# First cross attention of a gated Flamingo block in float32: keys projected turned, two heads in 32 rows, four heads' products side by side

## The chip, the cores and the metric

The kernel runs on one core of a Trainium2 chip. A core has the engines TensorE (PE, with its weight loads PEld), VectorE (DVE), ScalarE (ACT), GpSimd (POOL) and SyncE (SP), each with its own instruction queue, and 16 DMA engines. SBUF and PSUM have 128 partitions ("rows"); a PSUM bank holds 512 float32 per partition. A `matmul` keeps `lhsT` (rows x columns) in the array as weights and streams the columns of `rhs` past it; operands may occupy only a part of the rows (a row group) and the result a part of the partitions (a column group). `64*128` in a profile line means 64 rows by 128 columns of the array.

The metric is device time in microseconds, the median of several executions. Beside it stands one profiled execution with its trace, whose own time differs a little from the median.

## The reference

Four batches of 256 tokens `x` (256 wide) pass two gated blocks, each a cross attention to 1601 context tokens (128 wide) and a feed-forward part; each of the four sub-blocks is `x = x + tanh(g) * f(layernorm(x))`. Only the first cross attention is changed:

```
y_dca, y_main = y[:, -16:], y[:, :-16]                 # 16 and 1585 context tokens
q = ln16(x @ Wq + bq)                                  # 16 heads of 16
k = ln16(y_main @ Wk + bk);  v = y_main @ Wv + bv
k_dca = ln16(...);           v_dca = ...               # from y_dca @ Wkv_dca + bkv_dca
ctx = softmax(q k^T / 4) v + softmax(q k_dca^T / 4) v_dca
return ctx @ Wo + bo
```

`ln16` is a layer norm over the 16 numbers of one head, with one weight and one bias vector of 16 for all heads. The weight `kn_w` and the factor 1/4 are folded into the queries; `kn_b` gives the same number for every key of a query (`qc`). The second cross attention (16 query heads of 128, 8 key heads), the mixture of 16 experts and the ternary feed-forward block follow.

## The kernel before

Everything is computed on one core in order: a preamble, the first cross attention, the experts, the second cross attention and the last feed-forward block. The stages overlap a little at their borders.

**Units of the first cross attention.** The loop runs over 16 slabs: 4 batches (b) x 4 slabs (s) of 4 heads. A slab has 14 slots (`TILES`), one for each pair of 128-key chunks and each pair of heads (r = 0 or 2). The keys of a batch, turned (a head's dimensions on the rows, keys along the columns), are made while the batch before is attended to; the batch's own buffers `kTs`, `vps` alternate.

**Numbers in three parts.** Queries and keys are held as three bfloat16 parts (`NP` = 3), whose sum is the float32 number. A key's head takes 64 rows (`RW`): three times 16 rows of parts and a row of ones against which the queries' shift stands. A score is the sum of three bfloat16 products over 64 rows. Two heads stand in the two halves of the 128 rows.

**Keys.** `key_project` (L471) multiplies a chunk of 128 context tokens with `wkv`, keys and values together (512 columns); DVE adds the bias, ACT copies the values into `vps`. `scale_heads` squares on ACT (L373), sums and takes the root on DVE, and multiplies on POOL (L384); `split` makes the parts with ACT copies (L346, L350) and subtractions on POOL (L347, L351); `key_turn` (L516) turns each chunk by a DMA transpose on SP's queue, 13 per batch. For the first batch the same is done in the preamble by `first_pair` (L484), `parts` (L852) and their helpers.

**Queries.** `query_project`, the same steps on DVE and POOL, `stage_queries` (POOL copies at L615), and `turn_queries` (L625, one DMA transpose), twice per slab: once without the shift for the greatest pass, once with it.

**Greatest scores.** `greatest_tile` (L643) computes queries x 384 keys for two heads and reduces them to their greatest (L650, DVE), 16 tiles per slab, one slab ahead of the attention; `shift` writes qc minus the greatest sum into the shift rows.

**Attention.** `attend_tile` (L682) computes 256 keys x 256 queries for two heads into a `ps_s` tile of two PSUM banks (three such tiles exist, shared with the greatest pass), and ACT takes the exponential into `e` (L690, 1024 columns). `weigh` (L704) multiplies the values, 17 columns of 32 per head with a column of ones, with `e`: four heads in four column groups of one PSUM tile; it runs every second slot for two chunks. At a slab's end `take` (L720) copies the sums out, `norm` (L725 to L733) turns them and divides, and after the last slab of a batch `turn` (L742) and `out_project` (L749 on) apply `wo`. `last_tokens` (L565 to L606) does the 16 extra tokens.

**Order.** `keep_order` pins each engine to the order in which the program issues its instructions. In a slot that order is: one or two greatest tiles (`COUNT`), attend, exponential, every second slot weigh, and then the steps that `plan`, a dictionary from slot to steps, has for it. Slots for the helpers come from fixed tables (`KEYS`, `PARTS_AT` and numbers in `plan_queries`). In the last batch, which has no next batch's keys to make, `load_feed_forward` fetches the experts' weights and `route` picks experts for the batches done.

Of the kernel before, what the change touches and what calls it, by code (L numbers as in the profile page):

```python
# [21 lines left out]
P = 128  # L22
# [37 lines left out]
def tile_gated_cross_blocks(ctx: ExitStack, tc: tile.TileContext, a: dict, out: bass.AP):  # L60
# [192 lines left out]
    NS, HS, RW, W, NP = H // 4, 4, 64, 32, 3  # L253
    VW = HD0 + 1
    KPAD = NKT * P
    kt_stack = ExitStack()
    ktp = kt_stack.enter_context(tc.tile_pool(name="kt", bufs=1))
# [4 lines left out]
    kTs_f = [ktp.tile([P, H // 2 * KPAD // 2], F32, name=f"kT{i}") for i in range(2)]  # L262
    with ExitStack() as ph:
# [3 lines left out]
        hp = ph.enter_context(tc.tile_pool(name="l0h", bufs=2))  # L267
        qp = ph.enter_context(tc.tile_pool(name="l0q", bufs=2))
        ps_s = ph.enter_context(tc.tile_pool(name="l0ps_s", bufs=3, space=PSUM))
# [3 lines left out]
        groups = [[0, 1, 2], [3, 4, 5], [6, 7, 8], [9, 10, 11], [12]]  # L273
        GN = 3

        def load_group(b, gi):

            k0 = groups[gi][0] * P
            n = min(GN * P, NMAIN - k0)
            t = fix.tile([P, GN * P], F32, name="ctxg", bufs=4)  # L280
            nc.sync.dma_start(out=t[:, :n], in_=a["ctxT"][:, b, k0 : k0 + n])
            return t
# [3 lines left out]
        bkv = wp.tile([P, 2 * D], F32, name="bkv")  # L286
        nc.sync.dma_start(out=wkv[:, :D], in_=a["L0_xattn_Wk"])
        nc.scalar.dma_start(out=wkv[:, D:], in_=a["L0_xattn_Wv"])
        fetched = {(0, 0): load_group(0, 0)}
        nc.scalar.dma_start(out=bkv[:, :D], in_=a["L0_xattn_bk"].partition_broadcast(P))  # L290
        load_x(0)
        nc.scalar.dma_start(out=bkv[:, D:], in_=a["L0_xattn_bv"].partition_broadcast(P))
        load_x(1)
        fetched[0, 1] = load_group(0, 1)
        wq = load(wp, "wq0", [P, DC, D], a["L0_xattn_Wq"].rearrange("(c p) n -> p c n", p=P), nc.scalar)
        bq = bcast_row(wp, "L0_xattn_bq", D, nc.scalar)
        fetched.update({(0, gi): load_group(0, gi) for gi in range(2, 4)})
        hn = {
            n: bcast_row(wp, f"L0_xattn_{n}", HD0, nc.sync if "dca" in n else nc.scalar)
            for n in ("qn_w", "qn_b", "kn_w", "kn_b", "kn_dca_w", "kn_dca_b")  # L300
        }
        early = ph.enter_context(ExitStack())
        lp = early.enter_context(tc.tile_pool(name="l0last", bufs=1))
# [4 lines left out]
        bdca = bcast_row(lp, "bkv_dca", 2 * D)  # L308
        load_gates()
        wo = load(wp, "wo0", [P, DC, D], a["L0_xattn_Wo"].rearrange("(c p) n -> p c n", p=P))  # L310
        bo = bcast_row(wp, "L0_xattn_bo", D)
        for t in range(QT, NT):
            load_x(t)

        kTs = [t.bitcast(BF16).rearrange("p (c k) -> p c k", c=H // 2) for t in kTs_f]
        vps = [fix.tile([P, NKT, H * VW + W - VW], F32, name=f"vp{i}") for i in range(2)]
        kps = [fix.tile([P, GN, H, RW], BF16, name=f"kp{i}") for i in range(2)]
        kp_last = fix.tile([P, 1, H, RW], BF16, name="kp_last")
        qps = [fix.tile([P, NP, QT, HS, RW], BF16, name=f"qp{i}") for i in range(2)]
        nc.gpsimd.memset(kp_last, 0.0)  # L320
        for t, n in ((kps[0], P), (kps[1], P), (kp_last, TMAIN)):
            nc.gpsimd.memset(t[:n, :, :, NP * HD0 :], 0.0)
            nc.gpsimd.memset(t[:n, :, :, NP * HD0 : NP * HD0 + 1], 1.0)
        for t in qps:
            nc.gpsimd.memset(t[:, :, :, :, NP * HD0 :].rearrange("p n i h e -> p (n i h) e"), 0.0)

        def center(t3):

            g = t3.shape[1]
            sm = small.tile([P, 2 * H], F32, name="cen", bufs=2)  # L330
            nc.vector.reduce_sum(sm[:, :g], t3, axis=AX.X)
            nc.vector.tensor_scalar_mul(sm[:, :g], sm[:, :g], 1.0 / HD0)
            nc.vector.tensor_tensor(t3, t3, bc_last(sm[:, :g], HD0), ALU.subtract)
# [8 lines left out]
        def split(dsts, src, eng, first_eng=None):  # L342


            def first():
                nc.scalar.copy(dsts[0], src)  # L346
                (first_eng or eng).tensor_tensor(src, src, dsts[0], ALU.subtract)  # L347

            def second():
                nc.scalar.copy(dsts[1], src)  # L350
                eng.tensor_tensor(dsts[2], src, dsts[1], ALU.subtract)  # L351

            return [first, second]
# [12 lines left out]
        def scale_heads(src, n, g):  # L366

            sq = hp.tile([P, GN * H, HD0], F32, name="sq", bufs=1)
            v = small.tile([P, GN * H], F32, name="hn_var", bufs=2)[:n, :g]
            y, t = (small.tile([P, GN * H], F32, name=f"hn_{k}", bufs=1)[:n, :g] for k in "yt")  # L370

            def square():
                nc.scalar.activation(sq[:n, :g], src, AF.Square)  # L373

            def variance():
                nc.vector.reduce_sum(v, sq[:n, :g], axis=AX.X)
                nc.vector.tensor_scalar(v, v, 1.0 / HD0, 1e-6, ALU.mult, ALU.add)

            def root():
                log_root(v, y)  # L380
# [83 lines left out]
        def key_project(b, gi, ctxg, kns, i):  # L464
# [3 lines left out]
            if i == 0:  # L468
                kns[gi] = hp.tile([P, GN * H, HD0], F32, name="kn")
# [1177 lines left out]
```

## Time and profile before

| | us |
|---|---|
| median of 3 executions | 1617.81 (1617.75 to 1618.63) |
| profiled execution | 1620.98 |
| its span in the trace | 1619.3 |
| first exponential of the attention loop (L690) | 80.33 |
| last `take` (L720) of the first cross attention | 575.5 |
| from there to the end of the span | 1043.8 |
| mean granted TensorE clock | 0.981 |

The time from one `take` to the next, from first exponential on, adds up by batch to 142.4, 131.0, 127.0 and 94.9 us.

A page of the profile gives each engine's busy time in us, its share of the span and its instructions. A group line reads: line, engine, operation, output <- inputs, shapes, count | busy time, mean ns of one | idle time of the engine just before them and what ended it. A float32 matmul appears as two records, a bfloat16 one as one; records of matmuls overlap, since they are pipelined. A line of waits reads: engine and operation <- what it waited for: total us, times, longest us. A line of the chain of waits that ended last gives start, length, engine and line. A timeline line gives start, length, engine, line, operation, shapes, and in brackets the idle time before it.

### The profile page before, as it was taken

The numbers are of one execution on the slowest core, as the hardware profiler recorded it, in microseconds if no ns is written. First come the engines' busy times: TensorE is split into PE (matmuls) and PEld (weight loads), VectorE is DVE, ScalarE is ACT, GpSimd is POOL, SyncE is SP. The second block draws the span as 40 slices with busy tenths as digits, with TensorE's granted clock in tenths as the row PEclk, the third lists the DMA queues.
The fourth block names the chain that finished last, engine by engine and source line by source line (L and its number), as shares of the span: only waits on it lengthen the run. The fifth ranks groups of instructions, "written<-read, shape, count | busy, mean of one in ns | idle before, by whom it ended". The sixth has DMA issues, their size and how long they took to land.

```text
span 1619.3 us, 33935 instructions
## 1 busy us (share of the span) xinstructions
PE 1539.1 (95%) x13282; PEld 924.2 (57%) x13282; DVE 1159.3 (72%) x2615; ACT 798.9 (49%) x1852; POOL 601.7 (37%) x538
## 2 busy tenths in 40 slices
PE   4599999999999999989999999999999999999998
PEld 1354554554555545446666666666666666666665
DVE  6867677768767536687777777777777777777655
ACT  3256546556654634344455555544445454455343
POOL 4513213312401234434445444454444444444410
PEclk8799999999999989999999999999999999999999
DMA  4522414413442140000000000000000000000000
GB/s 113 110 45 48 73 33 68 83 26 54 84 87 54 41 166 1 1 2 9 8 16 15 15 9 15 9 22 2 15 15 9 22 9 15 9 2 3 2 0 27
DMA packets 148464, 54.04 MB, mean 33 GB/s; under 512 B 133200, under 2 KB 143952, under 8 KB 148176
## 3 DMA queue, kind: packets, MB, share of 16 engines
q1 hardware_dynamic: 134592, 50.65, 14.9%
q10 hardware_dynamic: 13712, 1.23, 0.6%
q8 instruction: 104, 1.70, 0.4%
q14 instruction: 56, 0.46, 0.1%
HBM read 24.30 MB, written 1.05 MB: 16 GB/s over the span
## 4 chain that ended last, share of the span: by engine, by line
PE 80%; DVE 11%; ACT 3%; issue 3%; POOL 2%; DMA 1%; ACTq 0%; SPq 0%; DVEq 0%; POOLq 0%
PE ps_o L1424 21%; PE ps_sc L1361 20%; PE ps_s L682 7%; PE ps_s L643 6%; PE ps_o L704 5%; PE ps_y L1442 4%; DVE mxs L650 4%; PE ps_m L1350 3%; PE ps_m L471 2%; PE ps_v L1184 2%; ACT pr L1376 1%; PE ps_a L1198 1%; PE ps_g L1555 1%; PE ps_x L1129 1%; PE ps_u L1555 1%
## 5 line engine op out<-in xcount | busy, mean ns | idle before, releaser
L1411 POOL TENSOR_TENSOR pr<-pr,rs 128x1604 f32<-128x1604 f32 x128 | 364.0, 2866 | 435.1 <-DMA rs<-ws 419.6
L1424 PE MATMUL ps_o<-pT,cx 128*128 128x256 f32 x1664 | 372.9, 382 | 7.8 <-DVE pT L1417 7.8
L1368 DVE CUSTOM_DVE_ANT_0 pr<-ps_sc,mk 128x401 f32<-128x401 f32 x512 | 294.7, 577 | 96.0 <-PE ps_sc L1361 57.3
L1361 PE MATMUL ps_sc<-ctxT,qT 128*32 128x401 f32 x4096 | 359.5, 502 | 0.5 <-DVE nm L1368 0.5
L1376 ACT ACTIVATE pr<-pr,nm 128x401 f32<-128x401 f32 x512 | 321.2, 628 | 71.2 <-DVE nm L1368 70.6
L1424 PEld LDWEIGHTS ps_o<-pT,cx 128*128 128x128 f32 x1664 | 318.9, 192 | 52.1 <-DVE pT L1417 8.5
L650 DVE TENSOR_REDUCE mxs<-ps_s 128x2 f32<-128x768 f32 (+1 forms) x256 | 245.5, 979 | 75.8 <-PE ps_s L643 75.2
L690 ACT ACTIVATE e<-ps_s 128x1024 f32<-128x1024 f32 (+1 forms) x224 | 214.7, 964 | 163.2 <-PE ps_s L682 150.5
L1417 DVE STREAM_TRANSPOSE pT<-pr 128x1664 f32<-128x1664 f32 x128 | 242.9, 1899 | 4.7 <-POOL pr L1411 4.7
L1361 PEld LDWEIGHTS ps_sc<-ctxT,qT 128*32 128x32 f32 x4096 | 126.4, 110 | 204.2 <-issue 118.6
L643 PE MATMUL ps_s<-kT,qTs 64*128 64x384 bf16 (+1 forms) x1536 | 173.7, 339 | 33.3 <-DMA qTs<-qp 18.1
L682 PE MATMUL ps_s<-qTs,kT 64*128 64x256 bf16 x2496 | 173.6, 270 | 9.5 <-DVE mxs L650 9.3
L682 PEld LDWEIGHTS <-kT 64*128 64x128 bf16 x2496 | 125.0, 94 | 54.9 <-issue 21.7
L643 PEld LDWEIGHTS <-qTs 64*128 64x128 bf16 x1536 | 65.2, 96 | 128.7 <-issue 82.0
L704 PE MATMUL ps_o<-e,vp 128*32 128x256 f32 x1664 | 112.6, 389 | 0.0
L1393 ACT ACTIVATE ws<-ws 32x32 f32<-32x32 f32 x64 | 14.6, 228 | 193.3 <-DVE ws L1392 193.3
L1434 ACT COPY ao<-ps_o 128x256 f32<-128x256 f32 x64 | 23.9, 373 | 152.8 <-PE ps_o L1424 141.4
L1376 ACT ACTIVATION_READ_ACCUMULATOR pr<-pr,nm 128x1 f32 x512 | 95.5, 186 | 0.0
L1442 PE MATMUL ps_y<-vo,ao 128*128 128x256 f32 x256 | 72.9, 408 | 1.9 <-ACT ao L1434 1.9
L1442 PEld LDWEIGHTS ps_y<-vo,ao 128*128 128x128 f32 x256 | 43.6, 190 | 46.3 <-ACT pr L1376 39.9
L704 PEld LDWEIGHTS ps_o<-e,vp 128*32 128x32 f32 x1664 | 44.6, 110 | 42.0 <-issue 24.7
L1350 PE MATMUL ps_m<-xnT,aq 128*128 128x256 f32 x256 | 65.8, 380 | 0.0
(287 smaller groups left out, 1507.3 us busy)
## 6 DMA issues: line engine op xcount, KB each, us to landing
ctxT<-in_ctxT_dram SPq DMA_DIRECT2D x4, 800.5 KB, 7.7
ctxg<-in_ctxT_dram SPq DMA_DIRECT2D x16, 192.0 KB, 3.1
kT<-in_L_xattn_Wq_dram SPq DMA_DIRECT2D x4, 512.0 KB, 3.6
wo<-in_L_xattn_Wo_dram SPq DMA_DIRECT2D x4, 512.0 KB, 4.8
bq<-nm SPq DMA_DIRECT2D x128, 2.0 KB, 1.7
bq<-nm ACTq DMA_DIRECT2D x128, 2.0 KB, 2.0
rs<-ws SPq DMA_DIRECT2D x128, 1.0 KB, 1.9
rs<-ws ACTq DMA_DIRECT2D x128, 1.0 KB, 1.8
```

The costliest lines, as they stand in the source:

```text
L643: nc.tensor.matmul(ps[:, k, :w], lhsT=qT[rows, j, i, r, :], rhs=kT[rows, 2 * s + r, c0 : c0 + w], start=j == 0, stop=j == NP - 1,)
L650: nc.vector.tensor_reduce(greatest_of[u][:, i, 2 * r : 2 * r + 2, n], ps[:, :, :w], AX.X, ALU.max)
L682: nc.tensor.matmul(ps[:, k, jj * S : (jj + 1) * S].rearrange("p (i q) -> p i q", i=QT), lhsT=kT[rows, 2 * s + r // 2, (j + jj) * P : (j + ...
L690: nc.scalar.activation(e[:, :, : nj * S], ps[:, :, : nj * S], AF.Exp)
L704: nc.tensor.matmul(summed[u][(r + k) * W : (r + k + 1) * W, :S], lhsT=vps[b % 2][:, j + jj, h * VW : h * VW + W], rhs=made[u, j, r][:, k, ...
L1361: nc.tensor.matmul(ps[i * TQ : (i + 1) * TQ, :KS], lhsT=queries[u][:, t * TQ : (t + 1) * TQ], rhs=ctxT[b][:, i * KS : (i + 1) * KS], start ...
L1368: nc.vector.tensor_tensor_reduce(out=prs[u % 3][:, t, :KS], in0=ps[:, :KS], in1=masks[b], scale=-1.0, scalar=3.0e38, op0=ALU.add, op1=ALU. ...
L1376: nc.scalar.activation(p, p, AF.Exp, bias=found[u][:, 0, t : t + 1], scale=-1.0, accum_out=found[u][:, 1, t : t + 1])
L1411: nc.gpsimd.tensor_tensor(p, p, bc_last(factors[:, ts], KS), ALU.mult)
L1417: nc.vector.transpose(pTs[u % 2][:, ts].rearrange("p t k -> p (t k)"), prs[u % 3][:, ts].rearrange("p t k -> p (t k)"))
L1424: nc.tensor.matmul(po[:, u % 2], lhsT=contexts[b][:, k, :], rhs=pTs[u % 2].rearrange("p t (k q) -> p t k q", q=TQ)[:, :, k, :], start=k == ...
L1442: nc.tensor.matmul(ys[b][:, i], lhsT=outs[u][:, i * P : (i + 1) * P], rhs=vo[:, h, :], start=(h, i) == (0, 0), stop=(h, i) == (H - 1, QT - 1),
```

## The change

Only the first cross attention and its preamble change (L250 to L1020); what follows is the same code.

- **Float32 throughout.** There are no parts: one float32 product over 16 dimensions takes the place of three bfloat16 ones over 64 rows. A head has 16 rows, two heads share 32 rows (even and odd slabs by turns, the other head's rows zeroed in the queries), and the four heads of a slab lie in four row groups.
- **Keys projected turned.** `key_product` (L472 after) has the centred weights `wk` stationary and up to 397 context tokens moving, so keys arrive with dimensions on the rows: eight products a batch. ACT squares them (`key_square`), ACT or DVE writes the raw keys (`key_raw`), `key_roots` (L502) sums squares by products with `hsum` and takes roots on DVE, `key_scale` (L525) spreads the roots over the rows by products with `sel`, and DVE multiplies. Values have their own products, `value_project` (L535). No DMA transposes remain.
- **Shift in a freed row.** Centred keys of a head add up to zero, so the 16th dimension can be dropped if it is subtracted from the queries' other 15 (`stage_queries`, L652 on); its row of keys is one and its row of queries the shift.
- **Queries turned by TensorE.** `turn_queries` (L664) is two PE transposes and an ACT copy.
- **Wider greatest tiles.** Three chunks of 453 keys and a rest of 226 keys for both query halves: 14 tiles per slab (L688), reduced at L697/L699.
- **Order in a slot.** attend (L732, two row groups), then a greatest tile of a slab ahead for the other two row groups, then the exponential (L742), then weigh for one 128-key chunk (L757, each slot), then the plan's steps. `book` gives at most one step that uses the `ps_m` tile to a slot; helpers are placed by it. `ps_s` still has three tiles; `e` has five (four before).
- **Preamble.** It does the keys of batch 0 by `first_keys`, then scales only the first half of the heads; the rest of the values and the extra tokens are interleaved with the first slab's greatest tiles. Context tokens are loaded whole, four DMAs per batch.

```diff
-    NS, HS, RW, W, NP = H // 4, 4, 64, 32, 3
+    NS, HS, W = H // 4, 4, 32
+    HW = H // 2
+    NG = 4
+    KG = (NMAIN + NG - 1) // NG
...
-    def key_project(b, gi, ctxg, kns, i):
-            nc.tensor.matmul(pm[:n], lhsT=ctxg[:, i * P : i * P + n], rhs=wkv, start=True, stop=True)
...
-    def key_turn(b, gi):
-                nc.sync.dma_start_transpose(
-                    out=kTs[b % 2][:, :, t * P : t * P + n],
-                    in_=parts_of(gi)[:n, i].rearrange("p h e -> p (h e)"),
-                )
+        def key_product(b, c, g, ps):
+            k0, n = GROUPS[g]
+            nc.tensor.matmul(ps[:, :n], lhsT=wk[:, c], rhs=ctxs[b][:, k0 : k0 + n], start=True, stop=True)
+        def key_square(c, g, ps):
+            nc.scalar.activation(sq[:, c, k0 : k0 + n], ps[:, :n], AF.Square, bias=kbias[:, c : c + 1])
+        def key_raw(b, c, g, ps, eng):
+            if eng is nc.scalar:
+                nc.scalar.activation(dst, ps[:, :n], AF.Identity, bias=rbias[:, c : c + 1], scale=n15)
+            else:
+                eng.tensor_scalar(dst, ps[:, :n], n15, rbias[:, c : c + 1], ALU.mult, ALU.add)
+        def key_roots(b):
+            for c in range(2):
+                for g in range(NG):
+                    nc.tensor.matmul(pm[g * W : (g + 1) * W, :KG], lhsT=hsum[:, c],
+                        rhs=sq[:, c, g * KG : (g + 1) * KG], start=c == 0, stop=c == 1)
+            nc.vector.tensor_scalar(v, pm[:, :KG], epsc, None, ALU.add)
...
+        def key_scale(b, c, half):
+            ps = ps_s.tile([P, 2, 512], F32, name="ps_s")
+            for i in range(2):
+                g = 2 * half + i
+                rows = slice(g * W, (g + 1) * W)
+                nc.tensor.matmul(ps[:, i, :KG], lhsT=sel[rows, c], rhs=roots[b][rows], start=True, stop=True)
+            nc.vector.tensor_tensor(k3, k3, ps[:, :, :KG], ALU.mult)
+        def value_project(b, t0):
+                nc.tensor.matmul(pm[:n, k], lhsT=ctxs[b][:, k0 : k0 + n], rhs=wv, start=True, stop=True)
...
-            nc.sync.dma_start_transpose(
-                out=t.rearrange("p n i r q -> p (n i r) q"), in_=qps[s % 2].rearrange("p n i h e -> p (n i h e)")
-            )
+        def turn_queries(u, k):
+            for i in range(QT):
+                nc.tensor.transpose(pt[:, i * P : (i + 1) * P], qps[slabs[u][1] % 2][:, i].rearrange(...), ident)
+            nc.scalar.copy(t, pt[:, :S])
...
-            for j in range(NP):
-                for k in range(2):
-                    rows = slice(k * RW, (k + 1) * RW)
+            for m, ii in enumerate([i] if whole else range(QT)):
+                for k in range(2):
+                    rows = slice((r + k) * W, (r + k + 1) * W)
...
-                for n in range(NP):
-                    for k in range(2):
-                        rows = slice(k * RW, (k + 1) * RW)
+                for k in range(2):
+                    rows = slice((r + k) * W, (r + k + 1) * W)
+                    nc.tensor.matmul(
+                        ps[:, k, jj * S : (jj + 1) * S],
+                        lhsT=kT[rows, s // 2, (j + jj) * P : (j + jj + 1) * P],
+                        rhs=qT[rows], start=True, stop=True)
+            def exponentials():
+                nc.scalar.activation(e[:, :, : nj * S], ps[:, :, : nj * S], AF.Exp)
...
-                for _ in range((COUNT if u else FIRST_COUNT)[k]):
-                    if todo:
-                        v, g = todo.pop(0)
-                        greatest_tile(v, *g)
-                attend_tile(u, k)
-                if k % 2 == 1 and k > 1:
-                    weigh(u, *PAIRS[k // 2 - 1])
-                run(plan, base_slot + k)
+                exponentials = attend_tile(u, k)
+                if ahead:
+                    v, _ = ahead.pop(0)
+                    next_greatest(v, 2 - TILES[k][2])
+                exponentials()
+                t = k - 2
+                if t >= 0:
+                    weigh(u, t)
+                elif t == -2 and u > 0:
+                    weigh(u - 1, NKT - 1)
+                for step in plan.pop(u * SLOTS + k, []):
+                    step()
```

## The prediction

> **What bounds the kernel now.** I read the page first: busy time, chain by line, groups. Its lines hold the whole program; only those at L643 to L704 belong to the 1st cross attention's loop.
>
> ```profile
> PE 1539.1 (95%) x13282; PEld 924.2 (57%) x13282; DVE 1159.3 (72%) x2615; ACT 798.9 (49%) x1852; POOL 601.7 (37%) x538
> ...
> L650 DVE TENSOR_REDUCE mxs<-ps_s 128x2 f32<-128x768 f32 (+1 forms) x256 | 245.5, 979 | 75.8 <-PE ps_s L643 75.2
> L690 ACT ACTIVATE e<-ps_s 128x1024 f32<-128x1024 f32 (+1 forms) x224 | 214.7, 964 | 163.2 <-PE ps_s L682 150.5
> ```
>
> Then the busy time of each engine by stretch: the preamble (up to the first exponential), the four batches, and all that follows. The columns are busy time and instructions of PE, PEld, DVE, ACT and POOL, then clock, DMA share and GB/s.
>
> ```profile
> 0.00:80.19 80.19, 41.04 (x206) 19.95 (x206) 58.19 (x99) 22.90 (x38) 41.38 (x84) 0.81 0.51 109
> 80.19:222.60 142.41, 132.22 (x1535) 72.12 (x1535) 101.87 (x195) 78.46 (x122) 32.57 (x52) 0.98 0.33 56
> 222.60:353.60 131.00, 125.83 (x1511) 69.17 (x1512) 97.66 (x189) 76.21 (x117) 33.15 (x54) 1.00 0.32 57
> 353.60:480.60 127.00, 122.79 (x1502) 67.97 (x1504) 95.07 (x180) 75.57 (x115) 32.45 (x53) 1.00 0.35 66
> 480.60:577.00 96.40, 94.77 (x1324) 57.82 (x1321) 53.75 (x128) 56.32 (x71) 16.05 (x35) 1.00 0.25 59
> 577.00:1619.30 1042.30, 1022.48 (x7211) 637.14 (x7210) 752.77 (x1828) 489.46 (x1389) 446.11 (x260) 0.99 0.06 15
> ```
>
> TensorE is busy 93 to 98% of the four batches: they are bound by its stream. The preamble is not: DVE, its busiest engine, works 58.2 of 80.2 us, and the clock is 0.81. The waits up to 80.2 us, longest first, say why:
>
> ```profile
> PE ps_s L643 <- DMA qTs<-qp: 18.1, 1, 18.1
> ...
> POOL kT L852 <- DVE v L364: 12.6, 2, 10.8
> ...
> PE ps_s L643 <- DMA kT<-kp: 3.6, 1, 3.6
> ```
>
> So 21.7 us of the preamble PE waits for DMA transposes. Last, the prices of products, from the chain around 730 us and the timelines at 641, 322 and 323 us:
>
> ```profile
> 729.28 5.53 PE ps_sc L1361 x64
> ...
> 735.86 5.61 PE ps_o L1424 x26
> ```
>
> ```profile
> 641.06 0.69 PE L1184 MATMUL ps_v<-xlT,kT 64*128 64x512 f32 x1
> ...
> 641.06 0.69 PE L1185 MATMUL ps_g<-xlT,kT 64*128 64x512 f32 x1
> ...
> 641.59 0.59 PE L1184 MATMUL ps_v<-xlT,kT 64*128 64x512 f32 x1
> ...
> 641.60 0.59 PE L1185 MATMUL ps_g<-xlT,kT 64*128 64x512 f32 x1
> ```
>
> ```profile
> 322.30 0.60 PE L682 MATMUL ps_s<-qTs,kT 64*128 64x256 bf16 x8
> ...
> 323.00 1.02 ACT L690 ACTIVATE e<-ps_s 128x1024 f32<-128x1024 f32 x1 [2.09 <-PE ps_s L682]
> 323.20 0.66 PE L643 MATMUL ps_s<-kT,qTs 64*128 64x384 bf16 x6
> ...
> 323.70 0.82 PE L682 MATMUL ps_s<-qTs,kT 64*128 64x256 bf16 x12
> ```
>
> A float32 product leaves two records. L1424's 26 records are 13 products of 256 columns: 5.61/13/256 = 1.69 ns per column. L1361's 64 are eight rounds of four 401-column products in four column groups: 0.69 a round, 1.72 per column, so four abreast cost what one does. L1184 and L1185, in two halves of the rows, begin together and take the same time: rows stand abreast as well. In bf16, twelve L682 products are six pairs, and less a record of 0.27 us, (0.82-0.27)/5 = 0.11 per pair; L643's three 384-wide pairs, (0.66-0.33)/2 = 0.16. An exponential starts 0.10 us after the last product's record ends (322.90 to 323.00).
>
> **The change: the stream.** Per batch, before: 624 L682 products are 312 pairs, 34.3 us; 384 L643 ones 192 pairs, 30.7; sum 65.0. After: attend (L732) is 104 float32 pairs of 256, 0.433 each, 45.0 us; the greatest pass (L688) 56 tiles of 453 columns, 0.766 each, 42.9. One behind the other that is 87.9, worse by 23. But attend takes two row groups and the greatest tile issued next the other two; abreast they would need about 45, better by 20. How far they overlap is set by the score buffer.
>
> **The change: the slot's wait.** Three buffers, two tiles per slot: the greatest tile of slot k takes the buffer of attend k-1, so it waits for that exponential. Attend is 0.107 (first load) + 2 x 0.433 = 0.97. Its exponential ends at 0.97 + 0.17 (record past stream, 0.27-0.11) + 0.10 + 1.02 = 2.26; PE goes on 0.16 after a ScalarE release (copy L595 ends 324.29, L599 starts 324.45). The greatest tile lasts 0.107 + 0.766 = 0.87. Weigh (L757) now comes each slot: switch of tile shape 0.09 + load 0.03 + 0.433 = 0.55, and 0.09 back (the gaps around L704 are 0.09). With m the inserted PE steps of a slot, slot k+1 begins m later than the later of a(k)+0.97+0.55+0.09 = a(k)+1.62 and a(k-1)+2.26+0.16+0.87+0.55+0.09 = a(k-1)+3.94. If the second always decides, a slot is 1.97 + m/2. Behind the waiting greatest tile stand weigh and all helpers on PE's queue; DVE and ACT then wait for them.
>
> **m.** Each step is load 0.107 + columns x 1.69 ns + switch 0.094. Per batch: key products 8 x 0.87 = 7.0, roots 1.5, four scale products 2.3, seven value steps 7.5, two query steps 2.1, new PE transposes of queries 8 x 0.42 = 3.4 (were DMAs), other transposes 10 x 0.42, last tokens 4.2, output 2.1: some 33, 0.6 per slot. Before, keys with values were 13 x 1.07 = 13.9, now 18.3; with the query transposes 7.8 us more PE work a batch, and 24 more visits to the weigh shape (52 for 28), 24 x 0.19 = 4.6 us. A slot is then 2.27 on average; carried slot by slot with each slot's own helpers (larger-of does not average) the batches come to 130.0, 129.6, 129.6 and 109.9 = 499.0. Before they were 142.4, 131.0, 127.0 and 94.9 to the last take at 575.5, sum 495.3. So the loop gets 3.7 slower: the first batch gains, where POOL's splits and DMA turns held up keys, and the last loses 15, since bf16 needs no second pass there and four rows abreast have no greatest tile beside them. The last slab, 23.6 by this, might be 20.5 if its exponentials run free; I leave it.
>
> **Other engines in the loop.** The reduce widens from 768 to 906 elements: L650 took 950 ns and, for 866 elements, 1057, so about 1.10, against 1.10/2.27 of the slot: hidden. Exponentials stay 1.02 of 2.27: hidden, except through the buffer. ACT gains squares, raw keys and query copies (0.37 each), POOL loses splits and copies: hidden by slack of 50% or more; if ACT's helpers run ahead of an exponential, it is late by 0.4, and half of that goes to its slot. SP loses 52 key and 32 query transposes, and its context loads become four a batch (five before), issued a slab or more ahead of use; at a DMA share of 0.33 nothing waits.
>
> **Preamble.** The DMA turns go (21.7 us of waits), the splits and most of POOL with them. Next late is DVE: 94 instructions, 47 us by the rows of before (18 greatest tiles 19.7). Bounds for the first exponential: 47 x 58.2/62.3 (its durations sum to 62.3) + the same 22 idle = 66; and 80, if the idle time comes back as waits on PE copies. I take 71, below their middle, since the waits that go are the longest: -9.
>
> **Tail.** L1 and the FFNs are unchanged, the 1043.8 us behind the last take stay; weights for the FFN are issued in the last batch before and after.
>
> **Sum.** -9 + 3.7 = -5.3. Span 1619.3 to 1614.0, the profiled execution 1621.0 to 1615.7; the median stands 3.2 below that execution: 1612.5.
>
> **A rule against it.** The trace has two row groups abreast, not four. It has four results at the same rate, though: an L682 pair yields two columns per 0.43 ns, four float32 tiles four per 0.85. So I take full overlap. The Trainium skill, "TensorE: Matmul & The Clock Gate", Part 3 (Packing small matmuls), gives 3.07 times, not 4, for four 32-row tiles of 512 columns. By it row tiles would be 30% slower, the recurrence would give 554 instead of 499, and the median would be about 1668; no row here shows it.
>
> **Rivals.** (1) Slower, the other side: four 32-row tiles are not fully abreast. For: never seen in this trace; against: the pair and the four column groups. In the recurrence 5% on L688 and L732 gives +9 (1622), 10% gives +18 (1631), pairs one after the other +113 (1726). Break-even is 3%. (2) The score buffer is freed later, because ACT helpers stand before the exponential or the release takes longer: 0.14 us per slot gives +9, 1622; for: ACT is busier per slot than the 58% of before; against: the idle time before L690. (3) No gain in the preamble: DVE's waits move to the PE turns; 1618 to 1621. (4) Cheaper: switches hidden under the buffer wait (0.05 instead of 0.094) give -19, 1593; no wait for the exponential at all -35, 1578, for which the fourth buffer is missing. (5) The change doesn't do what it says: TensorE keeps program order over row groups, so greatest and attend follow each other. The timeline at 598 us, where an L1185 of the next expert starts before an L1184 that precedes it, speaks against; it would be rival 1's +113.
>
> **How the numbers follow.** Forecast (1604 to 1616 by preamble bounds) 0.46; rival 4 0.14; rival 3 0.10; rivals 1 and 2 together 0.28, 5 0.02. Within 0.2% (3.2 us, about what a measurement of this kernel can tell from no change) lies rival 3 and the forecast's edge: same 0.13; faster 0.57; slower 0.30. The range drops the 35-us gain, the 30% case and serial pairs: 1593 to 1632.
>
> **What would show it.** Right: first exponential near 71 us with no DMA wait at the greatest tiles; exponentials 2.1 to 2.4 us apart; the last take near 570; PE in the greatest line waiting for ACT's e; L688 and L732 beginning together in four row groups; 1043.8 us after the last take. Wrong: L732 rounds longer than 0.433 per 256 columns when a greatest tile is beside them (rival 1), exponentials starting over 0.3 us after their products (rival 2), or a first exponential at 78 or later (rival 3).

## The result, and the profile after

The changed kernel takes 1617.26 us (median of 12, 1615.52 to 1624.2), the kernel before 1619.63 (12 executions, 1614.68 to 1623.44). The ratio, worked out over the single executions and not from the two medians, is 0.9995, with a 95% interval of 0.9979 to 1.0012: no difference that this measurement can tell. The forecast was 1612.5 us. The twelve executions of the changed kernel run from 1615.5 us at a mean granted clock of 0.983 (five of them within 0.5 us) to 1624.2 at 0.977, and the one profiled, at 0.978, is among the five longest.

That execution (1621.13 us, span 1619.4) shows that the equality is a sum of unequal parts:

| part | before, us | after, us | difference | forecast |
|---|---|---|---|---|
| up to the first exponential | 80.33 | 79.07 | -1.3 | -9 |
| first exponential to last take | 495.2 | 499.8 | +4.6 | +3.7 |
| behind the last take | 1043.7 | 1040.6 | -3.1 | 0 |

A second trace of the kernel before, at the end of the experiments, has 82.36, 491.9 and 1042.5 us; against it the differences would be -3.3, +7.9 and -1.9.

From the page of the changed kernel, busy times and the groups that answer to those of before:

```profile
PE 1566.6 (97%) x12200; PEld 915.5 (57%) x12200; DVE 1100.0 (68%) x2409; ACT 795.3 (49%) x1837; POOL 514.2 (32%) x424
...
L697 DVE TENSOR_REDUCE mxs<-ps_s 128x2 f32<-128x906 f32 x192 | 210.4, 1100 | 139.7 <-PE ps_s L732 70.0
L742 ACT ACTIVATE e<-ps_s 128x1024 f32<-128x1024 f32 (+1 forms) x224 | 215.2, 963 | 174.8 <-PE ps_s L732 156.3
...
L688 PE MATMUL ps_s<-kT,qT 32*128 32x453 f32 (+1 forms) x1024 | 232.3, 563 | 2.1 <-ACT e L742 1.2
```

The reduce takes 1.10 us, as worked out, and DVE and POOL lose work; TensorE gains 27 us of busy time, a part of it from products at half clock. By stretch (preamble, the four batches, the rest; columns as before):

```profile
0.00:79.07 79.07, 51.87 (x194) 24.74 (x196) 45.06 (x94) 19.88 (x39) 14.43 (x58) 0.74 0.26 74
79.07:212.66 133.59, 132.70 (x1246) 67.79 (x1246) 83.44 (x121) 77.01 (x113) 12.79 (x24) 0.96 0.03 7
212.66:342.13 129.47, 127.20 (x1242) 65.39 (x1243) 82.63 (x126) 75.77 (x110) 12.96 (x25) 1.00 0.01 1
342.13:471.61 129.48, 127.22 (x1242) 65.41 (x1244) 82.62 (x126) 75.77 (x111) 12.95 (x25) 1.00 0.04 10
471.61:578.85 107.24, 106.11 (x1073) 55.56 (x1071) 55.05 (x113) 59.30 (x76) 15.02 (x32) 1.00 0.11 32
578.85:1619.40 1040.55, 1021.49 (x7218) 636.62 (x7218) 751.21 (x1829) 487.58 (x1390) 446.09 (x260) 0.99 0.06 16
```

A batch is counted from its first exponential to that of the next, the last one to the last `take`, here as in the times by batch of the kernel before. The middle batches come to 129.5 us, where the recurrence, the prediction's slot-by-slot sum, said 129.6; the first to 133.6 (130.0), the last to 107.2 (109.9). In the preamble DVE and POOL are relieved as forecast (45.1 and 14.4 us of work), but TensorE's busy time *grew*, from 41.0 to 51.9, at a clock of 0.74 instead of 0.81. A finer cut shows where:

```profile
50.00:55.00 5.00, 3.12 (x15) 1.74 (x16) 4.79 (x9) 3.79 (x6) 1.83 (x3) 1.00 0.00 2
55.00:60.00 5.00, 4.23 (x16) 1.94 (x15) 1.15 (x2) 0.85 (x2) 2.84 (x9) 0.50 0.00 0
60.00:65.00 5.00, 4.32 (x22) 2.53 (x21) 1.84 (x5) 0.59 (x1) 1.32 (x6) 0.50 0.00 0
65.00:70.00 5.00, 3.50 (x13) 1.40 (x6) 3.51 (x9) 0.36 (x1) 0.00 (x0) 0.50 0.46 130
70.00:75.00 5.00, 4.00 (x16) 1.77 (x16) 0.72 (x1) 0.74 (x2) 0.00 (x0) 0.50 0.09 32
75.00:80.00 5.00, 5.00 (x24) 2.94 (x24) 4.08 (x5) 0.93 (x1) 0.00 (x0) 0.50 0.00 0
80.00:85.00 5.00, 5.00 (x26) 2.56 (x24) 2.58 (x3) 1.49 (x3) 0.00 (x0) 0.50 0.01 3
```

The granted clock is 0.50 from 55 us on; finer cuts have it back at 89.2. That takes in the last two of the seven rounds of the first slab's greatest tiles, the query turns, the second slab's first greatest tiles and the first four slots of the attention. The chain of waits says what came just before:

```profile
50.89 1.28 ACT L991
52.17 0.01 issue
52.18 0.21 ACT gate L991
52.39 0.02 issue
52.41 1.28 ACT L992
53.69 0.01 issue
53.70 0.59 ACT vp L536
54.30 0.04 issue
54.34 1.46 PE ps_m L535 x4
```

The gate's tanh, with a table load before and one after it (L991, L992), stands ahead of a value copy on ScalarE's queue. The value product L535 needs the bank that this copy frees, so TensorE stood idle for 1.88 us up to 54.34; the half clock begins at 55.0. That the one causes the other is only a theory so far.

Four row groups do stand abreast. The timeline of TensorE in a slot of the second batch:

```profile
243.80 0.48 PE L732 MATMUL ps_s<-qT,kT 32*128 32x256 f32 x2
243.82 0.65 PE L688 MATMUL ps_s<-kT,qT 32*128 32x453 f32 x2
244.12 0.38 PE L732 MATMUL ps_s<-qT,kT 32*128 32x256 f32 x2
244.31 0.55 PE L688 MATMUL ps_s<-kT,qT 32*128 32x453 f32 x2
244.33 0.60 PE L732 MATMUL ps_s<-qT,kT 32*128 32x256 f32 x4
```

All eight attend records precede the greatest tile's four in program order, yet L688 begins 0.02 us after the first L732 and before the other six. Attend and greatest tile end together after 1.1 us; one behind the other they would need 0.97 + 0.87 = 1.84.

### The profile page after: what moved, and what is told of

Same layout as the page of the kernel before. It is cut to its first block, busy times and chain, and to the rows that moved or that the text cites. A ratio compares the mean times of both kernels' runs of the same rounds, so it can differ in the third digit from the quotient of the medians.

```text
span 1619.4 us, 31284 instructions
## 1 busy us (share of the span) xinstructions
PE 1566.6 (97%) x12200; PEld 915.5 (57%) x12200; DVE 1100.0 (68%) x2409; ACT 795.3 (49%) x1837; POOL 514.2 (32%) x424
## 4 chain that ended last, share of the span: by engine, by line
PE 88%; DVE 4%; ACT 3%; issue 3%; POOL 1%; DMA 1%; ACTq 0%; SPq 0%; DVEq 0%; POOLq 0%
PE ps_o L1433 21%; PE ps_sc L1370 20%; PE ps_s L732 9%; PE ps_o L757 7%; PE ps_s L688 7%; PE ps_y L1451 4%; PE ps_m L1359 3%; PE ps_v L1193 2%; PE ps_m L535 2%; PE ps_m L472 1%; ACT pr L1385 1%; PE ps_a L1207 1%; PE ps_m L664 1%; DVE mxs L697 1%; PE ps_g L1564 1%
## 5 line engine op out<-in xcount | busy, mean ns | idle before, releaser
L697 DVE TENSOR_REDUCE mxs<-ps_s 128x2 f32<-128x906 f32 x192 | 210.4, 1100 | 139.7 <-PE ps_s L732 70.0
L742 ACT ACTIVATE e<-ps_s 128x1024 f32<-128x1024 f32 (+1 forms) x224 | 215.2, 963 | 174.8 <-PE ps_s L732 156.3
L732 PE MATMUL ps_s<-qT,kT 32*128 32x256 f32 x1664 | 240.1, 405 | 1.0 <-ACT e L742 0.9
L688 PE MATMUL ps_s<-kT,qT 32*128 32x453 f32 (+1 forms) x1024 | 232.3, 563 | 2.1 <-ACT e L742 1.2
L732 PEld LDWEIGHTS ps_s<-qT,kT 32*128 32x128 f32 x1664 | 142.2, 186 | 73.1 <-issue 39.7
L757 PE MATMUL ps_o<-e,vp 128*32 128x256 f32 x1664 | 134.3, 392 | 0.6 <-ACT e L742 0.6
L688 PEld LDWEIGHTS ps_s<-kT,qT 32*128 32x128 f32 x1024 | 80.1, 192 | 11.7 <-issue 3.8
L757 PEld LDWEIGHTS ps_o<-e,vp 128*32 128x32 f32 x1664 | 33.2, 108 | 91.0 <-issue 88.5
L788 POOL TENSOR_TENSOR ao<-ao,on 128x64 f32<-128x64 f32 x32 | 10.4, 326 | 228.5 <-DVE rs L783 168.2
```

What stands on the lines that cost most here:

```text
L688: nc.tensor.matmul(ps[:, k, m * w : (m + 1) * w], lhsT=qT[rows, ii * P : (ii + 1) * P], rhs=kT[rows, s // 2, n * CW0 : n * CW0 + w], start ...
L697: nc.vector.tensor_reduce(mx[:, i, r : r + 2, n], ps[:, :, :w], AX.X, ALU.max)
L732: nc.tensor.matmul(ps[:, k, jj * S : (jj + 1) * S], lhsT=kT[rows, s // 2, (j + jj) * P : (j + jj + 1) * P], rhs=qT[rows], start=True, stop ...
L742: nc.scalar.activation(e[:, :, : nj * S], ps[:, :, : nj * S], AF.Exp)
L757: nc.tensor.matmul(summed[u][(r + k) * W : (r + k + 1) * W, :S], lhsT=vps[b % 2][:, t, h * VW : h * VW + W], rhs=made[u, j, r][:, k, jj * ...
```

## The experiments

The theory: **the loop is what the recurrence says (four row groups abreast, the greatest tile waiting for the exponential of the slot before), and the preamble's gain was lost to TensorE's clock, which falls behind its idle stretches.** Rivals: the loop is bound by TensorE's stream or by partly serial row tiles; the preamble is bound by DVE and the order of steps whatever the clock.

The next three runs and the pairs of weigh near the end test the loop, the others the preamble. Each is the changed kernel with an edit, whose main lines are shown; some stand on top of an earlier run, as their expectations say. Where no count is given, the time is that of one execution. Executions of the changed kernel differ by up to 8.7 us, so these runs are read by the stretches of their traces and not by their totals. Their first loads land at different times, too: the last of the four groups of context tokens of batch 0 is projected (L472) at 19.36 us in the changed kernel, and between 19.3 and 22.1 us in the runs.

**Pairs on the same row groups.**

```diff
-                    next_greatest(v, 2 - TILES[k][2])
+                    next_greatest(v, TILES[k][2])
```

> Changed kernel, but the greatest tile issued after an attend tile is one for the same two row groups instead of the other two, so that the pairs can't stand abreast. My recurrence (four row groups fully abreast in the changed kernel): the loop from first exponential to last take grows from 499.8 us by 113, slabs of the second batch from 32.4, 33.4, 33.7, 29.9 to about 40.6, 42.2, 41.3, 37.4, the whole to about 1733. Rival (32-row tiles hardly overlap, 3.07 times for four): the pairs already cost about a third more than one, so the loss is smaller, 60 to 80 us, 1680 to 1700. If the loop's time is set by something else than these products: below 1650.

1736.61 us; the loop 612.4 us, 112.6 longer, against 113 forecast. Slabs of the second batch 40.1, 41.9, 40.7, 37.2. The timeline of a slot:

```profile
291.59 1.13 PE L732 MATMUL ps_s<-qT,kT 32*128 32x256 f32 x8
292.56 0.92 PE L688 MATMUL ps_s<-kT,qT 32*128 32x453 f32 x4
```

Now the greatest tile starts 0.97 us behind attend. The whole price of losing the side-by-side order appears, so the changed kernel had the whole of it: rival 1 of the prediction falls. The Trainium skill ("TensorE: Matmul & The Clock Gate", Part 3, Packing small matmuls) gives 3.07 times for four 32-row tiles. This case doesn't show that loss; a direct row stands at the pairs of weigh below.

**Half of each exponential** (the second chunk's exponentials are left out).

```diff
-                nc.scalar.activation(e[:, :, : nj * S], ps[:, :, : nj * S], AF.Exp)
+                nc.scalar.activation(e[:, :, :S], ps[:, :, :S], AF.Exp)
...
-                        rhs=made[u, j, r][:, k, jj * S : (jj + 1) * S],
+                        rhs=made[u, j, r][:, k, :S],
```

> Changed kernel, but each exponential takes only the first key chunk of its tile (512 columns instead of 1024), and weigh uses it for both chunks; the second chunk's exponentials are left out. TensorE's work stays the same. Recurrence (greatest tile waits for the exponential of the slot before, 1.02 us against 0.56): loop from 499.8 to about 475, total about 1592. Rival (the loop is bound by TensorE's stream alone): no change, 1615 to 1621. Rival (the exponential is what ends every slot): about 0.46 x 208 = 96 us less, 1521.

1598.08 us; loop 480.0, 19.8 shorter. Neither 0 nor 96: TensorE's own work is the same, and still the loop gets shorter by a fifth of what the exponentials lose (some 200 x 0.43 us). That is what a wait for the score buffer gives. It hardly shows as idle time: by the page's row of L688, the greatest tiles wait for an exponential for only 1.2 us in the whole program, so this run is the evidence for it. ScalarE's other work comes earlier here too, and the run does not separate that. The shorter exponential took 597 ns, not 0.56 us, which is part of the 5 us that are missing to the forecast of 475.

**Weigh every second slot.**

```diff
-                if t >= 0:
+                if t >= 0 and t % 2 == 1:
+                    weigh(u, t - 1)
                     weigh(u, t)
```

> Changed kernel, but weigh runs every second slot for two chunks, as in the kernel before: 24 switches to the weigh tile shape and 24 back fewer per batch. Stream theory (each switch costs 0.09 us of TensorE's time): 96 x 0.19 = 18 us less, 1599. Recurrence (a slot without weigh only waits longer for its score buffer, and the next is longer): loop 499.8 to about 518, total about 1636.

1630.6 us; loop 504.9, 5.1 longer. Fewer switches don't pay in the middle (second batch 132.9 against 129.5): the recurrence's direction (a slot without weigh only waits longer for its buffer), not the stream's 18 us less. But its size was missed: 5.1 us for 18. The first three batches lost 4.4, 3.4 and 3.4 us, and the last gained 6.0, since its last slab, where no greatest tile is left, fell from 21.7 to 15.3; the recurrence did not have that.

**Tanh early.**

```diff
-            if k == 2:
-                nc.scalar.activation(gate, gate, AF.Tanh)
-                nc.scalar.preload_act_table_set("natural_log_exp_and_others")
...
+        nc.scalar.activation(gate, gate, AF.Tanh)
+        nc.scalar.preload_act_table_set("natural_log_exp_and_others")
         for half in range(2):
             key_scale(0, 0, half)
```

> Changed kernel, but the gate's tanh and its two table loads on ScalarE move from the third round of the first slab's greatest tiles (50.9 to 53.7 us) to the stretch before the keys are scaled (about 26 to 29 us), where ScalarE stands idle. Clock theory (TensorE idles behind ScalarE there, the granted clock falls to 0.5 from 55 to 88 us, and all its work takes twice as long): the clock stays above 0.8 from 50 to 80 us, the first exponential comes at 64 to 72 instead of 79, the total falls by 7 to 17. Rival (the preamble is bound by DVE and by the order of the steps): the first exponential at 75 to 79, total 1614 to 1620.

1613.34 us, 7.8 below the profiled execution of the changed kernel. First exponential at 74.71, between the two forecasts; here the last context group was projected at 21.34 us, so that without this late start it would be near 72.7, just above the clock theory's range. The time from the first greatest tile to the shift fell from 31.2 to 26.0 us, the clock was 1.00 from 50 to 65 us, and fell to 0.50 again in the turns that wait for the shift; the first slab took 33.9 (34.5 in the changed kernel). Half of the theory's gain, then: with one idle stretch taken away the clock fell behind later ones (1.44 us up to 65.97).

**Values early.**

```diff
+        for _ in range(4):
+            value_project(0, next(values), True)
...
+        for t0 in values:
+            value_project(0, t0, True)
...
-            value_project(0, next(values))
```

> As e4_tanh_early, and the value products of batch 0 move out of the first slab's greatest rounds to the idle stretches of TensorE before them (between the roots and the first greatest tile), into score buffers. DVE theory (the greatest rounds are bound by DVE, 14 reduces of 1.10 us and the last tokens' steps, once nothing else stands between): rounds from 26 us to about 19, first exponential near 68. Clock theory: with fewer products in the rounds TensorE is busy less than half of the time, the clock stays at 0.5 through them and on to 16 us after the first attend, so that the first exponential comes near 70 to 73, and the first slab stays at 33 us or more against 30.7 of the recurrence at full clock.

1611.56 us; first exponential at 68.73, as the DVE theory had it, but with the clock that the other forecast: 0.58 from 40 to 50 us and 0.50 to 70. The greatest rounds took 22.6 us instead of 19, and the first slab 34.7. Undecided by itself. And the fall, at 41.7 us, did not come behind a long idle stretch: in the 3.4 us before it TensorE was busy for 2.77 and idle for 0.64 at most, with greatest tiles alone.

**Reordered, and reordered with idle stretches filled.**

```diff
-            value_project(0, next(values))
+            value_project(0, next(values), ps_o)
...
-        turn_queries(0, 1)
-        turn_queries(1, 0)
+            if k == HALF_SLAB - 2:
+                turn_queries(1, 0)
         for k in range(LEAD):
             next_greatest(1, (2, 0)[k % 2])
+            if k == 1:
+                turn_queries(0, 1)
```

> As e4_tanh_early, but the value products of the greatest rounds use the bank of the weighed sums, so that they no longer alternate with the last tokens' products in one bank, and the four greatest tiles of the second slab and its query turn are issued ahead of and around the turn that waits for the shift. Clock theory: no idle stretch of TensorE over 2 us from 45 us on, the clock stays at 1.0 past the first exponential, which comes near 66, and the first slab takes 31 to 32 us instead of 33.9: total near 1602. Rival (DVE and the order of steps alone): first exponential 70 to 72, first slab unchanged, total near 1610.

1616.48 us, a miss: first exponential 74.06, first slab 34.6. TensorE still waited for the last tokens' steps on POOL, and the clock, 1.00 from 45 to 55 us, was 0.72 from 55 to 60 and 0.50 behind that.

```diff
+        def keep_busy(n):
+            pd = ps_o.tile([P, 2, D], F32, name="ps_o")
+            for _ in range(n):
+                nc.tensor.matmul(pd[:, 0], lhsT=wk[:, 0], rhs=wkv[:, :D], start=True, stop=True)
...
+        keep_busy(8)
...
+        keep_busy(7)
```

> As e6_reordered, with 15 products added whose results nobody uses (256 columns each, 0.43 us at full clock), eight before the keys' scaling and seven before the queries' turn, in stretches in which TensorE of e4 waits for DVE. Clock theory: the clock does not fall below 0.9 between 25 and 45 us, the first two greatest rounds take about 5 us instead of 8.7, and the first exponential comes 3 to 4 us earlier than in e6. Rival (the granted clock follows something else than TensorE's idle time): clock of 30 to 45 us still 0.5, first exponential unchanged or up to 3 us later by the added work.

1612.83 us, first exponential 70.63: 3.4 earlier than without the 15 useless products, of which 0.6 is an earlier context (21.27 us for 21.91). The clock stayed at 1.00 from 25 to 50 us. The first two greatest rounds, from the first L688 to the third round's, took 5.1 us (7.2 without the useless products). Adding work brought the first exponential forward, as the clock theory says and the rival does not. From 52.9 us on the clock was at 0.50 again, behind a wait of 1.75 us for POOL up to 51.9.

**Rounds filled too** (values early, reordered, and useless products in each round).

```diff
+            keep_busy(3)
             next(last0, None)
+            if k == HALF_SLAB - 2:
+                turn_queries(1, 0)
```

> As e5_values_early, with three products of 256 columns whose results nobody uses in each of the seven greatest rounds of the first slab (1.3 us at full clock, ahead of the last tokens' step), and with the second slab's first greatest tiles around the query turn that waits for the shift, as in e6. The rounds of e5 lasted 22.6 us with the clock at 0.5 from 43 us on. Clock theory: the added work pays, since it keeps the clock: above 0.9 up to 70 us, rounds 19 to 20 us, the first exponential at 60 to 64 (e5 68.7), the first slab 31 to 32 us (e5 34.7), total 1600 to 1605. Rival (the clock's fall costs nothing here, DVE and the order set the pace): first exponential at 68 or later by the added 9 us of products, total 1611 to 1620.

1602.94 us. First exponential 65.76, 1.8 above the forecast's end; its context was projected 2 us later than in the changed kernel, and the rounds took 23.5 us, not 20, with TensorE waiting for the last tokens' steps on POOL again (1.32 us up to 52.45). The rest is as the theory had it:

```profile
50.00:55.00 5.00, 3.68 (x22) 2.21 (x20) 3.28 (x5) 0.27 (x1) 3.89 (x9) 1.00 0.01 2
55.00:60.00 5.00, 3.93 (x30) 2.63 (x28) 2.99 (x7) 0.37 (x1) 2.10 (x8) 1.00 0.00 0
60.00:65.00 5.00, 4.69 (x28) 2.22 (x28) 4.83 (x11) 0.37 (x1) 0.00 (x0) 1.00 0.02 3
65.00:70.00 5.00, 5.00 (x42) 2.53 (x38) 4.55 (x5) 2.42 (x3) 0.00 (x0) 1.00 0.00 0
```

At a clock of 1.00 from 40 us on, the first slab takes 30.4 us instead of 34.5 and the first batch 129.6 (130.0 forecast), with the other slabs unchanged. The 3.6 us that the first batch had over the forecast were the half clock. The earlier first exponential is not by the clock alone, since this run moves steps too.

**Filled alone: nothing moved.** The changed kernel with the useless products only, before the keys' scaling (8), before the queries' turn (7), in the rounds (2, and 6 in the fourth) and before the turn that waits for the shift (4).

```diff
+        keep_busy(8)
...
+        keep_busy(7)
...
+            keep_busy(6 if k == 3 else 2)
             value_project(0, next(values))
...
+        keep_busy(4)
         turn_queries(0, 1)
         turn_queries(1, 0)
```

> The changed kernel with nothing moved: products whose results nobody uses are added alone (256 columns, 0.43 us each at full clock): eight before the keys' scaling, seven before the queries' turn, two in each greatest round of the first slab and six in the fourth, where TensorE waited behind the table loads, and four before the turn that waits for the shift. Clock theory (the preamble's missing 8 us and the first batch's 3.6 us are TensorE at half clock): first exponential 66 to 72, near the 71 that I had predicted, first slab about 30.5, loop about 496, total 1603 to 1609, although 15 us of work are added. Rival (DVE, ScalarE and the order of steps): first exponential at 79 or later, total 1617 to 1630.

1613.85 us (5 executions), ratio to the kernel before 0.9958, interval 0.9944 to 0.9972, clear of the changed kernel's. The first exponential comes at 73.70, though some 16 us of products (37 of 0.43) were added; its context was projected 2.0 us late as well, and the forecast's 66 to 72 is missed by less than that. The clock is 1.00 from 40 to 70 us and falls only at the end:

```profile
50.00:60.00 10.00, 8.94 (x48) 5.84 (x46) 5.96 (x9) 4.04 (x7) 4.87 (x11) 1.00 0.00 1
60.00:70.00 10.00, 8.18 (x50) 5.31 (x52) 4.40 (x13) 1.44 (x4) 1.13 (x6) 1.00 0.27 83
70.00:80.00 10.00, 9.55 (x52) 4.87 (x48) 7.32 (x7) 2.42 (x3) 0.00 (x0) 0.67 0.00 0
```

With that late fall the first slab took 34.7 and not 30.5, most of the 5 us by which the total missed its range. The fall itself goes against the theory as far as its trigger: it came at 73.5, after 3.4 us in which TensorE was busy for 2.96 and idle for 0.45 at most, with greatest tiles and the first attend, all of 32 rows. With its start at the changed kernel's, the first exponential would stand at about 71.7, where the prediction put it. The rival, 79 or later, is out: by this estimate the clock cost the preamble about 7 us.

**Pairs of weigh in the last two slabs,** on top of the filled rounds.

```diff
-                if t >= 0:
+                if t >= 0 and u < len(slabs) - 2:
                     weigh(u, t)
+                elif t >= 0 and t % 2 == 1:
+                    weigh(u, t - 1)
+                    weigh(u, t)
```

> As e8_rounds_filled, and weigh takes two chunks every second slot in the last two slabs alone, where e3_pair_weigh was faster (25.5 and 15.3 us against 26.3 and 21.7): there no greatest tile waits for an exponential, and only the switches of tile shape remain. Expected: 7 us less than e8 in the last batch, elsewhere the same; 1593 to 1600 and a ratio to the kernel before of 0.986 to 0.990. Rival (what e3 gained at the end belonged to the earlier slabs' order): the last batch as in e8.

1596.41 us (5 executions, 1592.27 to 1597.61), ratio to the kernel before 0.9847, interval 0.9831 to 0.9862: faster than both kernels. The last batch took 100.1 us, 7.2 less than with the rounds filled; last slabs 25.5 and 15.3. My reason for it was wrong, however. In the last slab six switches there and back fewer are worth 6 x 0.19 = 1.1 us, and it got 6.4 shorter. The timeline of TensorE in the last slab shows the rest:

```profile
541.72 1.13 PE L732 MATMUL ps_s<-qT,kT 32*128 32x256 f32 x8
542.78 1.07 PE L757 MATMUL ps_o<-e,vp 128*32 128x256 f32 x16
543.78 1.16 PE L732 MATMUL ps_s<-qT,kT 32*128 32x256 f32 x16
544.87 1.07 PE L757 MATMUL ps_o<-e,vp 128*32 128x256 f32 x16
```

Sixteen L732 records, the attends of both head pairs, take 1.16 us; the eight of one attend alone, in the first line, take 1.13. With no weigh between them two attends stand abreast, in four row groups, for the price of one. That is also the row that speaks to the skill's 3.07: four 32-row float32 tiles took 1.16/1.13 = 1.03 of the time of two. By the figure of that page ("TensorE: Matmul & The Clock Gate", Part 3) four tiles would take an estimated 4/3.07 = 1.3 times as long as one; its tiles are 512 columns wide, these 256.

**Both kernels once more,** for second traces.

> The kernel before, unchanged, for a second trace of it. In the first the stretch behind the last take lasted 1043.7 us, in the ten traces of the changed kernel and its variants 1037.3 to 1041.9, with the same code. If that stretch only varies from execution to execution: anywhere between 1037 and 1044 here. If the change reaches into it: 1043 or more again.

> The changed kernel, unchanged, for a second trace of it. Clock theory and recurrence: first exponential 79 to 81 (2 us later where the first loads land later), the clock at 0.5 from about 55 to 88 us again, loop 499 to 501 us, and the second and third batch at 129.4 each again. If the fall of the clock was an accident of one execution: a first exponential of 70 to 74 and a first slab near 30.5.

Before: first exponential 82.36, loop 491.9, behind the last take 1042.5. Changed: 79.08, 499.8, 1040.4, with batches of 133.5, 129.5, 129.5 and 107.2 and the clock at 0.50 from 55 to 85 us again. The three runs that test the loop first, whose preamble is the changed kernel's, show it as well, so the half clock is no accident of one execution. All these traces have a mean clock of 0.980 or less, though; of those at 0.983 there is no trace. By that mean they had some 16 us less at half clock (0.005 x 1617/0.5, an estimate), and whether in the preamble is open. The preamble and first batch of before vary by 2.0 and 3.3 us between its two traces. What stands behind the last take has the same code everywhere: 1043.7 and 1042.5 in two traces of before, 1037.3 to 1041.9 in twelve of the changed kernel and its variants. The spread goes with the clock: the two shortest (1037.3 and 1037.6) spend 14 us of that stretch at 0.50, the other ten 18 to 27. Both traces of before have 3.4 us at 0.50 near 1533 us that none of the twelve has. Whether the change reaches that far or chance does it, two traces can't tell; it stays open.

## Why the prediction was right and wrong

**The stream, the slot's wait, m.** Right. The loop took 499.8 us for 499.0. The second and third batch took 129.5 us each against 129.6. Of its two disputed mechanisms, four row groups abreast was shown by an edit of its own (112.6 us for 113); the wait for the exponential of the slot before is supported by another (19.8 us for 24.8), though the sign that the prediction named for it, greatest tiles seen waiting for `e`, is nearly absent (1.2 us). Its direction held with fewer switches too, its size did not (5.1 for 18). The exactness of the sum is partly luck: the first batch was 3.6 us over, by the half clock, and the last 2.7 under, of which the last slab's 1.9 is in the direction that the prediction named and left out. The terms of m add up to 34.3, not to "some 33"; both are 0.6 per slot.

**Preamble.** This step failed: -9 forecast, -1.3 measured (-3.3 against the second trace of before). Its terms held (45 us of DVE work, no DMA wait at the greatest tiles), but it took DVE to be next and gave TensorE's own steps no price (only the bound of 80 lets idle time come back "as waits on PE copies"), so none for their taking twice as long at a clock of 0.50. The row of the stretch before, 58.2 of 80.2 us of DVE and 0.81 of clock, had the clue in its last columns. The change took away DVE and DMA waits and put more of TensorE's products, with single-bank handovers to ScalarE, into the place. At half clock they became the bound; with it kept up to 70 us, in the run with nothing moved, some 7 us came back. What sets off a fall is shown only in part: most fell behind idle time of TensorE, two did not. Rival 3 had the outcome (first exponential at 78 or later, 1618 to 1621) and a neighbouring reason, "waits on PE turns"; the clock was not named.

**Tail.** 0 forecast, -3.1 in the profiled execution, against a spread of 4.6 us in this stretch over twelve traces of the same code. By luck it cancelled most of the loop's loss.

**Sum.** With -1.3 and +4.6 the forecast would have been 1621 in place of 1612.5; with the tail's -3.1, and a median that stands 3.9 below the profiled execution instead of 3.2, it comes to 1617.3. The median of 1617.26 lies inside the range, and within 0.2%, to which 0.13 was given. The forecast's "1604 to 1616 by preamble bounds" does not follow from its bounds: 66 and 80 us give 1607.5 to 1621.5.

**Rivals.** 1 (row tiles not fully abreast) is refuted by the same-rows run and by the 16 records in 1.16 us. 2 (later buffer release) did not occur by the batch times; half an exponential is worth 20 us of the loop. 4 (cheaper switches) did not occur in the loop. 5 falls with the timeline at 243.8 us: products of other row groups start ahead of earlier ones.

## What to carry to other kernels

Carry a slot recurrence with each buffer's release written into it: it gave the two middle batches to within 0.2 us at full clock, and the sign, not the size, of an edit (fewer switches, yet slower) that a sum of busy times gets wrong. Before pricing a start-up or any stretch with gaps, read the granted clock of it; where it is below 1, ask which idle stretch of TensorE comes first, and move the work that causes it, since the price can last: here 34 us behind an idle stretch of 1.88. Products over 32 rows are worth ordering so that neighbours lie in different row groups with no other tile shape between them.

## What the runs showed of the hardware

- Cut into half microseconds at both ends of the slow stretch, TensorE's granted clock in the changed kernel was 0.50 or 1.00, save in the cut in which it changed. It fell at 55.0 us, behind an idle stretch of 1.88 us, and came back only at 89.2, although no cut of five microseconds from 75 us on shows TensorE idle. The Trainium skill ("TensorE: Matmul & The Clock Gate", Part 1, the clock gate) has it come back after about 3.4 us of sustained work. The two levels agree with that page; the return took at least 14 us here.
- In the clock records of all fourteen traces, a stretch at one clock lasts a multiple of 3.41 us, save the last one, which ends with the program (17.07, 10.24 and 34.13 in the changed kernel's first 89 us). Of 33 falls in the first 100 us, 31 came at the end of such 3.41 us in which TensorE was busy for at most 0.52 of them (0.45 before the fall at 55.0). The two others (0.81 at 41.7 us with the values early, 0.87 at 73.5 us filled alone) came while TensorE ran products over 32 rows alone. That such products count for less is a guess that no run here tests.
- Some 16 us of useless products made a kernel faster by 3.4 us in the median (1613.85 for 1617.26).
- Two attends of two 32-row float32 tiles each took 1.16 us side by side, one alone 1.13.
